# A token's own head of keys and values, by blocks of rows, in a routed attention layer

## The chip, the cores and the metric

The kernel runs on one core of a Trainium2 chip. Its metric is the device time of one execution in microseconds (us); the time before is the median of three runs. One more execution was recorded by the hardware profiler, and its rows are quoted here. PE is the matrix engine (TensorE), PEld its loading of weights, DVE the vector engine, ACT the scalar engine, POOL GpSimd, SP the engine that issues most transfers. SBUF is the on-chip memory, PSUM the accumulators that PE writes to.

## The reference

A decoder of two layers works on `x` of 8 sequences × 256 tokens × 512 features, in float32: 2048 tokens, 16 tiles of 128. After each sublayer comes the residual sum and a layer norm. The first layer has differential attention, a long convolution and a mixture of experts; the second has windows of self attention, cross attention to a context, and the sublayer of this case:

```python
gating = softmax(x @ W_gate.T)                   # 16 gates, one for each head
idx = argmax(gating); indicator = one_hot(idx, 16)
gating_top1 = indicator * max(gating)
q, k, v = split(x @ W_qkv.T, 3)                  # 16 heads of 32 features each
k_shared = einsum('bth,bthd->btd', indicator, k)     # the token's own head of k
v_shared = einsum('bth,bthd->btd', gating_top1, v)   # the same head of v, times its gate
att = einsum('bhqd,bkd->bhqk', q, k_shared) / sqrt(32)
y = einsum('bhqk,bkd->bhqd', softmax(causal(att)), v_shared)
```

Each token has 16 heads of queries, and one head of keys and values, whose number its gate chooses.

## The kernel before

`x` stays in SBUF as 16 tiles of 128 tokens × 512 features. `D` is 512, `KB` = 4 its chunks of 128, `P` = 128; a group is 4 tiles (512 tokens, two sequences), and `NG` = 4 groups are worked off one after another. A matmul 128×512 in float32 runs as two passes, so it has two records in the profile. `project` (L171) and `product_steps` (L182) issue the 4 matmuls of a product; `transpose` (L165) and `turned` (L194) turn a tile by 4 transposes and one copy.

**The mixture of experts** (`experts`) sorts tokens: a router chooses, POOL scatters the rows to a DRAM buffer `xs` by slots that are counted out per expert (L782), PE works on blocks of 128 rows whose expert's weights are addressed by a register (loaded at L915), and the results are gathered.

**Cross attention** (`cross_attention`, L1548 to L1633) does per group: 4 tiles turned, `seven_tokens` (sums of quarters of the turned tokens), three times `seven_products` (q, k, v; 7 products of 4 matmuls 128×256 instead of 8), and then the attention of two sequences, which a pipeline works off in pieces beside the next group's products.

**Routed attention** (`routed_attention`, L1642 to L1739) gives its parts to `causal_attention` (L1097 to L1402), whose order is written out by hand and not by a scheduler. It has 32 units (4 for each sequence, 8 for each group, each unit 4 of the 16 heads). A unit's steps are: `maxima` (12 matmuls `ps_q`, L1151; ACT copies them to `rows`, L1160; POOL masks them, L1162; DVE takes maxima, L1171); 5 units later `weights` (`ps_k`, L1214; ACT's exp to `pT`, L1231; POOL masks and adds, L1232 and L1242); 6 units later `products` (`ps_pv`, L1257 and L1267; DVE's reciprocal L1275 and product L1281). `ps_q` and `ps_k` share one PSUM tile. After a sequence's four maxima, DVE splits them into bfloat16 terms and PE turns them (`ps_n`, L1193). Between these steps `fill` puts pieces of work from a queue sorted by the unit in which they are due, at 0.86 us per matmul (`MM`) and 0.45 per turned tile (`TR`); `need` puts in what is due; `at(slots, place, f)` puts a step at the start, middle or end of a later unit. `begin(g)` calls `prepare` for the next group in the middle of the group before, for group 0 before the first unit.

`prepare` queues per group: 4 tiles turned to `xT`; the gates of the 4 tiles (`ps_g`, 16 matmuls of 16 columns, then DVE's softmax and first maximum); 4 blocks of q (`ps_f`, 16 matmuls 128×512); and for each tile **all 16 heads** of k and of v (`ps_t`, two products of 4 matmuls 128×512). From each `ps_t` DVE picks the token's own head, in `chosen`: a product with the indicator (L1676) and a sum over the heads (L1682). k is repeated four times (L1687) and turned (`keys_turned`, L1692).

Of the kernel before, what the change touches and what calls it, by code (L numbers as in the profile page):

```python
# [16 lines left out]
F32 = mybir.dt.float32  # L17
# [6 lines left out]
P = 128  # L24
# [21 lines left out]
NE = (PH * 2 * P - E * (P - 1) - 1) // P + 1  # L46


@with_exitstack
def decoder_kernel(ctx: ExitStack, tc: tile.TileContext, a: dict, out: bass.AP):  # L50
# [43 lines left out]
    ctx_d = dram.tile([P, KB, B * S], F32, tag="ctx_d", name="ctx_d")  # L94

# [101 lines left out]
    def turned_group(work, pools, g):  # L197

        xT = []

        def step(ti):
            if ti == 0:
                xT.append(work.tile([P, KB, GT], F32, tag="xT", name="xT", bufs=1))
            turned(pools, xT[0][:, :, ti * P : (ti + 1) * P], x[g * TPG + ti])

        return xT, [(0, [(TR, lambda ti=ti: step(ti))]) for ti in range(TPG)]
# [7 lines left out]
    class Pipeline:  # L214
# [3 lines left out]
        def __init__(self):  # L218
            self.steps = []
# [392 lines left out]
    def experts(rt):  # L612
# [480 lines left out]
        return clear_slots, load_experts, load_gu_last, router, blocks, combine, wide  # L1093
# [3 lines left out]
    def causal_attention(name, prepare, finish, upb=KB, gather=None):  # L1097
# [18 lines left out]
        with ExitStack() as st:  # L1116
# [177 lines left out]
            def at(slots, place, f):  # L1294

                if place == "fill":
# [210 lines left out]
    def seven_tokens(work, xT):  # L1507

        (b11, b21), (b12, b22) = quadrants(xT)
        t = work.tile([P, 4, 2, S], F32, tag="ts", name="ts", bufs=1)  # L1510
        nc.vector.tensor_tensor(t[:, 0], b12, b11, ALU.subtract)
        nc.gpsimd.tensor_tensor(t[:, 2], b22, b12, ALU.subtract)
        nc.vector.tensor_tensor(t[:, 1], b22, t[:, 0], ALU.subtract)
        nc.vector.tensor_tensor(t[:, 3], b21, t[:, 1], ALU.subtract)
        return b11, b21, t[:, 1], t[:, 2], t[:, 3], t[:, 0], b22

    def seven_products(work, pools, weights, tokens, dst, token_major=False):
# [3 lines left out]
        def product(n):  # L1521
            ps = pools.tile([P, 2, S], F32, tag="mm", name="ps_7")
            rows, cols = (tokens, weights) if token_major else (weights, tokens)
            for i in range(2):
# [5 lines left out]
                )  # L1530
            return ps
# [4 lines left out]
        p1, u2, u3 = part("p1"), part("u2"), part("u3")  # L1536
# [3 lines left out]
        add(u2, product(2), p1)  # L1540
        add(u3, product(3), u2)
# [6 lines left out]
    def cross_attention(wq, wk, wv, wo):  # L1548
# [52 lines left out]
        with ExitStack() as st:  # L1601
# [7 lines left out]
            for g in range(NG):  # L1609
# [13 lines left out]
                seven_products(work, pools, wq7, x7, lambda i, l: q[l][i])  # L1623
# [3 lines left out]
                seven_products(work, pools, wk7, x7, lambda i, l: k[l][i])  # L1627
                v = work.tile([P, TPG, D], F32, tag="v", name="v_x", bufs=1)
                vq = quadrants(v)
                seven_products(work, pools, wv7, x7, lambda i, l: vq[i][l], True)  # L1630
# [11 lines left out]
    def routed_attention(wqkv, wg):  # L1642

        idx = index_row(const, H1, "idx_h")

        def prepare(work, pools, g, at, here):
# [5 lines left out]
            k4 = work.tile([P, TPG, 4, HD1], F32, tag="k4", name="k4")  # L1652
            ind = work.tile([P, TPG, H1], F32, tag="ind", name="ind")
            itop = work.tile([P, TPG, H1], F32, tag="itop", name="itop")

            def gates():
                ps = pools.tile([P, TPG, H1], F32, tag="mm", name="ps_g")
                for ti in range(TPG):
                    project(
                        ps[:, ti, :],  # L1660
                        lambda k: xT[0][:, k, ti * P : (ti + 1) * P],
                        lambda k: wg[:, k, :],
                    )
                gate = work.tile([P, TPG, H1], F32, tag="gate", name="gate")
                nc.vector.tensor_copy(gate, ps)
                softmax_small(work, gate, H1)
                top = work.tile([P, TPG], F32, tag="top", name="top")
                first_max(work, gate, H1, idx, top, ind)
                nc.vector.tensor_tensor(
                    itop, ind, top.unsqueeze(2).broadcast_to([P, TPG, H1]), ALU.mult  # L1670
                )

            def chosen(dst, ps, by):

                sel = work.tile([P, H1, HD1], F32, tag="sel", name="sel")
                nc.vector.tensor_tensor(  # L1676
                    sel,
                    ps.rearrange("p (h d) -> p h d", d=HD1),
                    by.unsqueeze(2).broadcast_to([P, H1, HD1]),
                    ALU.mult,  # L1680
                )
                nc.vector.tensor_reduce(dst, sel.rearrange("p h d -> p d h"), AX.X, ALU.add)  # L1682

            def key(ti, ps):
                k = k4[:, ti]
                chosen(k[:, 0, :], ps, ind[:, ti, :])
                nc.vector.tensor_copy(k[:, 1:4, :], k[:, 0:1, :].broadcast_to([P, 3, HD1]))  # L1687

            def keys_turned():
                pt = pools.tile([P, TPG, P], F32, tag="mm", name="pt_k")  # L1690
# [6 lines left out]
            xT, need = turned_group(work, pools, g)  # L1697
            need.append((0, [(0.8, gates)]))
            need.append((0, feature_block(pools, qT, xT, wqkv, 0, 0, HD1**-0.5)))
            for ti in range(TPG):  # L1700
                need.append(
                    (0, token_block(pools, xT, wqkv, D, ti, lambda ps, ti=ti: key(ti, ps)))
                )
            for c in range(1, 3):
                need.append((0, feature_block(pools, qT, xT, wqkv, 0, c, HD1**-0.5)))
            need.append((0, [(TR, keys_turned)]))
            for c in range(3, KB):
                need.append((c, feature_block(pools, qT, xT, wqkv, 0, c, HD1**-0.5)))
            for ti in range(TPG):
                need.append(  # L1710
                    (
                        5 + ti // 2 * (4 if g == NG - 1 else 2),
# [142 lines left out]
```

## Time and profile before

| | us |
|---|---|
| median of 3 runs (2217.38 to 2219.33) | 2218.76 |
| the profiled execution, its own time | 2202.62 |
| its span | 2200.8 |
| cross attention | about 1548 to 1843 of the span |
| routed attention, to the first `ps_q` | 1843 to 1876 |
| units 0 to 4 | 1876.0 to 1895.8 |
| units 5 to 12 | 1895.8 to 1975.3 |
| units 13 to 31 | 1975.3 to 2155.3 |
| rest | 2155.3 to 2200.8 |

A page of the profile gives each engine's busy time and share of the span, then the span in 40 slices (a digit is the busy share in tenths). Groups of instructions stand as line, engine, operation, `out<-in` with shapes and count, then busy us, mean ns of one, and the idle time of the engine just before them with what ended it. A timeline's line is start, duration, engine, line and operation, with the idle time before in brackets.

### The profile page before, as it was taken

What the parts mean: (1) busy time and instruction counts of PE and PEld (TensorE: products, weight loads), DVE (VectorE), ACT (ScalarE), POOL (GpSimd) and SP (SyncE); (2) the same over time, 40 slices, a digit from 0 to 9 for tenths busy, and PEclk for the clock granted to TensorE, in tenths of its full rate; (3) what the DMA queues carried; (4) which work ended last, traced back from release to release, by engine and by line L of the source; (5) the groups of instructions that cost most, each with busy time, mean ns of one, the idle gap of its engine ahead of it and who ended that gap; (6) DMA issues with size and microseconds to landing.
All of it is one profiled execution on the core that took longest, in us unless ns stands there. A gap on an engine that the chain in (4) does not pass through costs nothing. (4 is left out here: it accounts for less than half of the span.)

```text
span 2200.8 us, 35612 instructions
## 1 busy us (share of the span) xinstructions
PE 2053.4 (93%) x14904; PEld 1192.7 (54%) x14904; DVE 1272.1 (58%) x1923; ACT 598.9 (27%) x723; POOL 824.4 (37%) x918
## 2 busy tenths in 40 slices
PE   7989899879999999999959999999999999999995
PEld 4545555544453455555524444446877875445543
DVE  4676767758888964222235746466344343476777
ACT  4545545520010013111114333340110110333342
POOL 2566767737556723000033644343000000242343
PEclk9989999989999999999989999999999999999998
DMA  6899801335124144131140201002100100000000
GB/s 221 328 385 382 312 1 45 92 87 198 29 76 164 29 148 149 62 141 61 48 145 29 77 20 58 1 2 96 39 20 20 39 0 1 1 11 11 11 18 33
DMA packets 110032, 197.56 MB, mean 90 GB/s; under 512 B 7088, under 2 KB 30768, under 8 KB 109872
## 3 DMA queue, kind: packets, MB, share of 16 engines
q1 hardware_dynamic: 104752, 178.49, 23.4%
q0 software_dynamic: 5120, 16.78, 2.2%
q8 instruction: 120, 1.97, 0.4%
q14 instruction: 40, 0.33, 0.0%
HBM read 93.54 MB, written 112.20 MB: 93 GB/s over the span
## 5 line engine op out<-in xcount | busy, mean ns | idle before, releaser
L1275 DVE RECIPROCAL rsum<-ps_pv 128x256 f32<-128x256 f32 x128 | 224.4, 1753 | 238.1 <-PE ps_pv L1267 237.9
L171 PE MATMUL ps_y<-kv,wt 128*128 128x512 f32 x640 | 282.6, 600 | 4.4 <-POOL kv L519 3.8
L1231 ACT ACTIVATE pT<-ps_k 128x1536 f32<-128x1536 f32 x128 | 185.7, 1450 | 288.9 <-PE ps_k L1223 286.9
L1171 DVE TENSOR_REDUCE neg<-rows 128x12 f32<-128x1536 f32 x128 | 223.1, 1743 | 50.9 <-POOL rows L1162 50.9
L1160 ACT COPY rows<-ps_q 128x1536 f32<-128x1536 f32 x128 | 184.2, 1439 | 184.0 <-PE ps_q L1151 142.2
L1162 POOL TENSOR_SCALAR_AFFINE_SELECT rows<-rows 128x1024 f32<-128x1024 f32 x128 | 140.1, 1094 | 250.3 <-ACT rows L1160 250.0
L1232 POOL TENSOR_SCALAR_AFFINE_SELECT pT<-pT 128x1024 f32<-128x1024 f32 x128 | 141.1, 1102 | 242.9 <-ACT pT L1231 242.9
L171 PEld LDWEIGHTS ps_y<-kv,wt 128*128 128x128 f32 x640 | 120.9, 192 | 154.4 <-issue 135.8
L1242 POOL TENSOR_TENSOR pT<-pT 128x512 f32<-128x512 f32 x112 | 145.2, 1296 | 9.3
L1077 POOL DMA_INDIRECT w_l1x<-ys,slots x32 | 32.9, 1028 | 267.1 <-DMA ys<-y_m 259.2
L182 PE MATMUL ps_t<-w_l1f,xT 128*128 128x512 f32 x256 | 122.0, 611 | 0.0
L182 PE MATMUL ps_f<-xT,w_l1a 128*128 128x512 f32 x256 | 118.2, 604 | 2.9 <-ACT xT L195 2.9
L992 PE MATMUL po_m<-dn,hT 128*128 (+1 forms) x216 | 101.9, 609 | 1.5
L139 POOL TENSOR_SCALAR rstd<-bn_mv 128x1 f32<-128x1 f32 x80 | 16.9, 212 | 217.0 <-DVE bn_mv L145 211.2
L1267 PE MATMUL ps_pv<-pT,ones_v 128*32 128x256 f32 (+1 forms) x1152 | 85.0, 377 | 6.7 <-POOL pT L1242 6.3
L557 DVE TENSOR_REDUCE yc<-z 128x64 f32<-128x512 f32 x128 | 86.0, 673 | 6.2 <-POOL w_l1a L558 5.8
L1151 PE MATMUL ps_q<-kz,qT 32*128 32x128 f32 x1536 | 62.9, 294 | 22.6 <-ACT pT L1231 17.5
L1151 PEld LDWEIGHTS ps_q<-kT,qT 32*128 32x128 f32 x1536 | 49.9, 190 | 56.2 <-issue 17.0
L1151 PEld LDWEIGHTS ps_q<-kz,qT 32*128 32x128 f32 x1536 | 50.4, 192 | 54.8 <-ACT pT L1231 34.4
L182 PEld LDWEIGHTS ps_f<-xT,w_l1a 128*128 128x128 f32 x256 | 46.3, 189 | 54.8 <-issue 49.3
L1151 PE MATMUL ps_q<-kT,qT 32*128 32x128 f32 x1536 | 62.4, 292 | 12.5 <-ACT kT L1411 4.8
L974 DVE TENSOR_TENSOR h_b<-h_b,pg 128x352 f32<-128x352 f32 x36 | 18.8, 521 | 95.3 <-ACT h_b L973 95.3
(326 smaller groups left out, 3744.6 us busy)
## 6 DMA issues: line engine op xcount, KB each, us to landing
xs<-zero SPq DMA_DIRECT2D x8, 4352.0 KB, 31.3
ys<-zero SPq DMA_DIRECT2D x8, 4352.0 KB, 31.4
filters<-in_L_xattn_k SPq DMA_DIRECT2D x4, 2560.0 KB
first_h<-xs SPq DMA_DIRECT2D x36, 256.0 KB, 2.6
ys<-y_m SPq DMA_DIRECT2D x36, 256.0 KB, 2.0
gu<-in_L_ffn_gate_up_proj SPq DMA_DIRECT2D x3, 2816.0 KB, 19.8
wt<-filters SPq DMA_DIRECT2D x32, 256.0 KB, 2.8
x<-in_x SPq DMA_DIRECT2D x16, 256.0 KB, 4.9
```

The costliest lines, as they stand in the source:

```text
L171: nc.tensor.matmul(ps, lhsT=lhsT(k), rhs=rhs(k), start=(k == 0), stop=(k == n - 1))
L182: nc.tensor.matmul(ps[0], lhsT=lhsT(k), rhs=rhs(k), start=(k == 0), stop=(k == KB - 1))
L557: nc.vector.tensor_reduce(yc[:, lb], z, AX.X, ALU.add)
L992: nc.tensor.matmul(po, lhsT=hT[:m, i, :], rhs=dn[i][:m, bass.ds(e, 1), :], start=(i == 0), stop=(i == len(FCH) - 1),)
L1151: nc.tensor.matmul(block[:, s, j, :], lhsT=q(rows, c, b * S + i * P, P), rhs=k(rows, c, b * S + keys * P, P), start=True, stop=True,)
L1160: nc.scalar.copy(d.rearrange("p j s k -> p s j k"), block)
L1162: nc.gpsimd.affine_select(out=rows, in_=rows, compare_op=ALU.is_ge, fill=-FAR, base=0, pattern=[[0, 8], [-1, P]], channel_multiplier=1,)
L1171: return lambda: nc.vector.tensor_reduce(neg[u // upb % 2][:, :, :, c], d, AX.X, ALU.max, negate=True)
L1231: nc.scalar.activation(p[:, 0:3].rearrange("p j s q -> p s j q"), block, AF.Exp)
L1232: nc.gpsimd.affine_select(out=p[:, 0:2].rearrange("p j s q -> p (j s) q"), in_=p[:, 0:2].rearrange("p j s q -> p (j s) q"), compare_op=ALU ...
L1242: nc.gpsimd.tensor_tensor(p[:, 3], p[:, 1], p[:, 2], ALU.add)
L1275: nc.vector.reciprocal(r, ps[:, 1, :])
```

## The change

Keys and values are no longer formed for all heads. Tokens are sorted by their head in two halves of 8 tiles, as in the mixture of experts: a half's rows go to `xs`, in slots that are filled up to blocks of 128 rows of one head each (8 + 15 = 23 blocks, `NKB`). A block is turned and multiplied by the 64 columns of k and v of its head, which a register selects; the results go to a DRAM buffer `kv_d` and are gathered back by token. A new class `Heads` does this:

- `gate`: a tile's 16 gates, and a copy of them on DVE. `choose`: softmax, first maximum and running sums. `places`: three small matmuls (`ps_pl`) and some 15 small operations on DVE that make slots, and the head of each block.
- `send`: a scatter of a tile on POOL. Only the first half's are declared independent of one another.
- `blocks`: a list of 25 steps, of which step b turns block b+2 (`pt_h`), loads block b's head into a PE register and multiplies block b (`ps_kv`); 8 blocks share a PSUM tile, one copy and one transfer. `ahead` buffers are loaded in advance by SP.
- `gather`: a tile's k and v from `kv_d` on POOL.

The first half runs in cross attention: gates after the k products of groups 1 and 2, `choose`, `places` and `send` after those of group 2, and one step of `blocks(ahead=2)` after each of the 21 products of group 3 (`between`); the four steps that remain and the gathers follow. The second half runs in the units of group 0 of routed attention: gates due in units 1 to 3, `choose` in unit 3, `places` in unit 4, sends in units 5 to 7, blocks (`ahead=5`) due in units 9 to 13, gathers in units 13 to 16. `ps_t` and `chosen` are gone; `keys_turned` repeats k by a copy on ACT and multiplies v by its gate on DVE. In `seven_tokens` a difference is formed in place, on POOL and after another on DVE, and in `seven_products` `u3` takes the buffer of `p1`.

On all engines the order before cross attention is as it was. PE's instruction count, as the compiled orders list it, goes from 4879 to 5335, DVE's from 1867 to 1828, ACT's from 629 to 665, POOL's from 848 to 878.

```diff
+NKB = PH + H1 - 1
...
+    kv_d = [dram.tile([NKB * P, 2 * HD1], F32, tag=f"kv{i}", name=f"kv{i}") for i in range(2)]
...
             def at(slots, place, f):
 
-                if place == "fill":
+
+                if place == "due":
+                    at(slots, "start", lambda: insort(queue, f, key=lambda piece: piece[0]))
+                elif place == "fill":
...
-        t = work.tile([P, 4, 2, S], F32, tag="ts", name="ts", bufs=1)
+        t = work.tile([P, 3, 2, S], F32, tag="ts", name="ts", bufs=1)
         nc.vector.tensor_tensor(t[:, 0], b12, b11, ALU.subtract)
-        nc.gpsimd.tensor_tensor(t[:, 2], b22, b12, ALU.subtract)
         nc.vector.tensor_tensor(t[:, 1], b22, t[:, 0], ALU.subtract)
-        nc.vector.tensor_tensor(t[:, 3], b21, t[:, 1], ALU.subtract)
+        nc.gpsimd.tensor_tensor(b12, b22, b12, ALU.subtract)
+        nc.vector.tensor_tensor(t[:, 2], b21, t[:, 1], ALU.subtract)
...
+            between()
             return ps
...
+                steps = []
+                if g == NG - 1:
+                    steps = half.blocks(work, pools, evacuate, 2)
...
+                if 0 < g < NG - 1:
+                    for ti in range(TPG):
+                        xt = work.tile([P, KB, P], F32, tag="xT_b", name="xT_g")
+                        transpose(pools, xt, x[(g - 1) * TPG + ti], "mm")
+                        half.gate(pools, (g - 1) * TPG + ti, lambda k: xt[:, k, :])
+                if g == NG - 2:
+                    half.choose()
+                    half.places(pools)
+                    half.send(range(PH))
...
-                seven_products(work, pools, wv7, x7, lambda i, l: vq[i][l], True)
+                seven_products(work, pools, wv7, x7, lambda i, l: vq[i][l], True, between)
+                if g == NG - 1:
+                    while steps:
+                        between()
+                    for t in range(PH):
+                        half.gather(t)
...
+        def gate(self, pools, t, xT):
+            ps = pools.tile([P, H1], F32, tag="mm", name="ps_g")
+            project(ps, xT, lambda k: self.wg[:, k, :])
+            nc.vector.tensor_copy(self.logits[:, t - self.first, :], ps)
...
+        def send(self, tiles):
+            for i in tiles:
+                ins = nc.gpsimd.indirect_dma_start(
+                    out=xs[:, :],
+                    out_offset=bass.IndirectOffsetOnAxis(ap=self.slots[:, i : i + 1], axis=0),
+                    in_=x[self.first + i],
+                    in_offset=None,
+                )
+                if self.first == 0:
+                    tc.declare_no_dep(ins.ins, group="heads", reason="every token has its own slot")
+                    tc.add_to_no_dep_group("heads", ins.ins)
...
+        def blocks(self, work, pools, copy, ahead=5):
+            xb, xT, out = {}, {}, []
+            def load(b):
+                if b < NKB:
+                    xb[b] = work.tile([P, D], F32, tag="xb_h", name="xb_h", bufs=ahead)
+                    nc.sync.dma_start(out=xb[b], in_=xs[b * P : (b + 1) * P, :])
+            def turn(b):
+                if b < NKB:
+                    pt = pools.tile([P, KB, P], F32, tag="mm", name="pt_h")
+                    for k in range(KB):
+                        nc.tensor.transpose(pt[:, k, :], xb[b][:, k * P : (k + 1) * P], ident)
+                    xT[b] = work.tile([P, KB, P], F32, tag="xT_b", name="xT_h", bufs=min(3, ahead))
+                    copy(xT[b], pt)
+                    del xb[b]
+                    load(b + ahead)
+            def step(b):
...
+                turn(b + 2)
+                e = nc.values_load(
+                    self.heads[0:1, b : b + 1],
+                    engines=(mybir.EngineType.PE,),
...
+                for k in range(KB):
+                    nc.tensor.matmul(
+                        out[-1][:, b % 8],
+                        lhsT=xT_b[:, k, :],
+                        rhs=self.w[:, k, bass.ds(e, 1)],
+                        start=(k == 0),
+                        stop=(k == KB - 1),
+                    )
+                n = b % 8 + 1
+                if n == 8 or b == NKB - 1:
+                    y = work.tile([P, 8, 2 * HD1], F32, tag="sc", name="kv_b")
+                    copy(y[:, :n], out.pop()[:, :n].rearrange("p b a d -> p b (a d)"))
...
+            return [lambda b=b: step(b) for b in range(-2, NKB)]
...
-            for ti in range(TPG):
-                need.append(
-                    (0, token_block(pools, xT, wqkv, D, ti, lambda ps, ti=ti: key(ti, ps)))
-                )
...
-            for ti in range(TPG):
-                need.append(
-                    (
-                        5 + ti // 2 * (4 if g == NG - 1 else 2),
-                        token_block(
-                            pools, xT, wqkv, 2 * D, ti,
-                            lambda ps, ti=ti: chosen(v[:, ti, :], ps, itop[:, ti, :]),
...
+            if g == 0:
+
+                other = halves[1]
+                other.rows_for(work)
+                for n in range(2, NG):
+                    late[n], turns = turned_group(work, pools, n, f"xT{n}")
+                    for ti, (_, steps) in enumerate(turns):
+                        t = n * TPG + ti
+                        tokens = lambda k, n=n, ti=ti: late[n][0][:, k, ti * P : (ti + 1) * P]
+                        gate = lambda t=t, tokens=tokens: other.gate(pools, t, tokens)
+                        need.append((n - 1 + ti // 2, steps + [(0.9, gate)]))
+                at(3, "mid", other.choose)
+                at(4, "fill", [(0.4, lambda: other.places(pools))])
+                for i in range(PH):
+                    at(5 + i // 3, ("start", "mid", "end")[i % 3], lambda i=i: other.send([i]))
+                steps = other.blocks(work, pools, nc.scalar.copy)
+                for i, f in enumerate(steps):
+                    at(8, "due", (9 + i * 5 // len(steps), [(1.3 if i > 1 else TR, f)]))
+                for i in range(PH):
+                    at(13 + i // 2, ("mid", "end")[i % 2], lambda i=i: other.gather(PH + i))
```

## The prediction

> **What bounds the kernel now.** I read the totals of the page first, then a table of windows by stage, then the groups by tile and shape inside the routed stage, then the waits and the timeline there. The totals:
>
> ```profile
> span 2200.8 us, 35612 instructions
> PE 2053.4 (93%) x14904; PEld 1192.7 (54%) x14904; DVE 1272.1 (58%) x1923; ACT 598.9 (27%) x723; POOL 824.4 (37%) x918
> PE   7989899879999999999959999999999999999995
> ```
>
> PE is busy for 93% of the span, so a matmul less is a gain only if the stage it leaves stays PE-bound, and a matmul more is a loss wherever it is put into a full stage. The windows (columns: length, then busy us and records of PE, PEld, DVE, ACT, POOL; granted PE clock, DMA share, GB/s) are the MoE blocks of layer 0, the end of cross attention, and five parts of the routed stage:
>
> ```profile
> 905.00:1095.00 190.00, 189.34 (x662) 111.89 (x661) 45.82 (x91) 32.92 (x70) 0.00 (x0) 1.00 0.23 81
> 1700.00:1843.00 143.00, 139.87 (x606) 109.37 (x604) 52.76 (x96) 15.83 (x34) 7.69 (x17) 1.00 0.05 15
> 1843.00:1875.00 32.00, 30.50 (x97) 15.71 (x98) 10.88 (x27) 4.58 (x9) 0.00 (x0) 0.95 0.00 1
> 1975.00:2155.00 180.00, 173.45 (x1682) 93.20 (x1674) 131.23 (x179) 63.23 (x60) 67.70 (x70) 0.96 0.04 14
> 2155.00:2201.00 46.00, 24.06 (x382) 14.46 (x378) 34.02 (x49) 10.52 (x8) 16.37 (x23) 0.80 0.09 35
> ```
>
> Every stretch but the tail is full on PE. What fills it in the routed stage, and what DVE does there:
>
> ```profile
> L182 PE MATMUL ps_t<-w_l1f,xT 128*128 128x512 f32 x256 | 122.0, 611 | 0.0
> L1275 DVE RECIPROCAL rsum<-ps_pv 128x256 f32<-128x256 f32 x32 | 56.0, 1751 | 33.5 <-PE ps_pv L1267 33.3
> L1171 DVE TENSOR_REDUCE neg<-rows 128x12 f32<-128x1536 f32 x32 | 55.8, 1742 | 12.5 <-POOL rows L1162 12.5
> L1682 DVE TENSOR_REDUCE k<-sel 128x32 f32<-128x512 f32 x16 | 16.6, 1040 | 0.5
> ```
>
> The 256 records are the two passes of 128 matmuls `ps_t` (16 tiles, k and v, 4 chunks). The records overlap; start to start one matmul takes 0.86 us, so they hold 128×0.86 = 110 us of PE.
>
> **The sum's base.** The profiled execution took 2202.62 us (span 2200.8); the median of the runs is 2218.76, 16.1 us more. I work out a difference against the profiled one and add it to the median.
>
> **Cost of one gate and one block.** The MoE router does what a new gate does, 4 transposes of a tile and 4 matmuls of few columns:
>
> ```profile
> 804.94 0.97 PEld L171 LDWEIGHTS ps_r<-rw,w_l1a 128*128 128x128 f32 x8
> 805.93 0.42 PEld L724 LDWEIGHTS pt_c<-ident,w_l1a 128*128 128x128 f32 x4
> 806.31 0.97 PEld L171 LDWEIGHTS ps_r<-rw,w_l1a 128*128 128x128 f32 x8
> 807.26 0.44 PE L194 MATMUL pt<-ident,first_h 128*128 128x128 f32 x2
> ```
>
> From 805.93 to 807.26 is 1.33 us for both: 0.45 of transposes and 8 weight loads of 0.112, so few columns do not make it shorter. A block of 64 columns is the same form: 1.33 us. It also loads its head into a PE register, as the MoE does 36 times (ns: least, median, most):
>
> ```profile
> L915 PEldq TENSOR_LOAD <-i_ex x36: 297/302/786, 792.5 to 1094.7; - x36
> ```
>
> With 4 register operations of 0.05 that is 0.50 us. In the MoE window above these stand among full PE work and PE is busy 189.34 of 190, so I take them as hidden; if open, a block is 1.83. With turn, copy to SBUF and loads all open it is 0.45+0.9+0.9+0.5 = 2.75.
>
> **Cross attention (+46).** 8 gates and 23 blocks go into a stage where PE was busy 139.87 of 143: 31×1.33 = 41.2. Three `ps_pl` matmuls 0.5, and they stand in PE's order behind DVE's chain of small operations in choose: 2. The 4 steps for which the 21 products have no gap stand alone: each waits for its load (the MoE's 256 KB blocks landed in 2.6 us, a step is 1.33): 2. Hidden: block loads and copies, since a step and a product (1.33+1.73) lie between issue and use, twice; the 8 sends on POOL (0.96 each, busy 7.69 of 143) and gathers (3.6 to landing), needed only in routed attention; the POOL subtraction in seven_tokens that now waits for DVE's. The `u3` that reuses p1's buffer waits for an add already done. Range +41 (no waits) to +58 (23×0.5 open).
>
> **To the first ps_q (−22.5).** 32 us before: 16 `ps_g`, 16 `ps_t`, 12 `ps_f` matmuls. After: 4 tiles turned (1.8) and one feature block (3.44), keys_turned (0.45), 5.7 in all, and the copies that PE waits for, of the last turned tile, q, k four times over and kT (0.6 to 0.9 each with hand-over), 3.8: about 9.5.
>
> **Units 0 to 4 (+23).** Before 19.8 us (1876.0 to 1895.8). They now carry 8 turns and gates of the second half (10.6), the first group's other 12 `ps_f` (10.3) and the rest of the next unit's work; each gate stands on PE behind ACT's copy of its own turn (0.5 plus hand-over, 0.9 in all: 7.2 for 8), `ps_pl` behind choose (2.8). The 10 `ps_t` that stood here are gone (9.0). So 19.8+10.6+10.3+7.2+2.8−9.0 = 41.7, and 1 for the first batch's split and turn, which have less work around them: 42.7. Range +12 (waits covered) to +27.
>
> **Units 5 to 12 (+5.5).** Before 79.5 us (1895.8 to 1975.3). Gone are 33 `ps_t` (65 records of the tile in this window, 28 us); added are 23 blocks (30.6). The sends of this half are not declared independent, so each waits on POOL for the landing of the one before: 2.7 us in the MoE's scatters, whose issues otherwise follow at 1.27 (839.71, 840.98). Behind them in POOL's order stand the selects of `rows` and `pT` (1.10 each), for which DVE's maxima and PE's `ps_pv` wait, and the last send releases the first block load on SP. About 10 us of wait over four units, partly covered. Range −8 to +18.
>
> **Units 13 to 31 (−68).** Before 180 us (1975.3 to 2155.3), PE busy 173.45. Gone are 68 `ps_t` (135 records, 58 us), 32 `ps_g` (two groups, 32×0.112×2 = 7.2) and 8 turned tiles (3.6): PE keeps about 105. Another bound lies close to that: the one score tile passes from `ps_q` (0.95) to ACT's copy (1.44), `ps_k`, ACT's exp (1.45) and back. The timeline of ACT shows four units of the forecast's kind already in this profile, between two groups' products:
>
> ```profile
> 2033.24 1.44 ACT L1160 COPY rows<-ps_q 128x1536 f32<-128x1536 f32 x1 [1.44 <-PE ps_q L1151]
> 2039.34 1.44 ACT L1160 COPY rows<-ps_q 128x1536 f32<-128x1536 f32 x1 [1.28 <-PE ps_q L1151]
> 2045.46 1.44 ACT L1160 COPY rows<-ps_q 128x1536 f32<-128x1536 f32 x1 [1.30 <-PE ps_q L1151]
> 2051.56 1.44 ACT L1160 COPY rows<-ps_q 128x1536 f32<-128x1536 f32 x1 [1.28 <-PE ps_q L1151]
> ```
>
> 6.1 us from copy to copy. DVE needs 1.75+1.74+0.42 per unit and about 1.4 of norms and split, 5.35, less than that. 18 units of 6.2, the products spread over them, are 112. Range −75 (5.85 each) to −55 (6.9).
>
> **Tail (−8).** Before 45.5 us; DVE was late there (PE waited 4.59 us for `terms`), among others with `chosen` for v. Range −10 to −2.
>
> **Sum.** 46−22.5+23+5.5−68−8 = −24: 2218.76−24 = 2195.
>
> A rule of the Trainium skill speaks against it: "DMA: Bandwidth & Descriptors", section "Latency and other measured facts", gives a floor of about 600 ns for a tensor_load. This case's row shows a median of 302 ns on PE. By the page 46 exposed loads would be 27.6 us, an estimate that takes the whole gain; by the row they would be 13.9, and hidden, nothing.
>
> **Rivals.** (1) *Waits covered (faster still).* If the gates' copies, choose and the scatter chain are hidden by the units' other work, units 0 to 12 cost +4 (the low ends) instead of +28.5: −48, 2171. For: PE was busy 78.33 of 80 there and the schedule fills gaps. Against: the order on PE is fixed by hand and a gate stands right behind its turn. (2) *Register work just open.* 46×0.5 = +23, sum −1: 2218, no change. Against: the MoE window. (3) *Slower: a block costs more than its tensor time.* In the MoE a register load came once in 8.4 us of PE work (36 from 792.5 to 1094.7), here once in about 3, and at the four steps that stand alone once in 1.3. At +0.52 per block (24/46) the gain is gone, so this decides from 1.85 a block on; at 2.75 a block, 1.42 more than the forecast's 1.33, the sum is 46×1.42−24 = +41, 2260. (4) *Light units do not speed up*: if DVE or the score chain holds 8 us per unit, −68 becomes −36 and the sum +8, 2227. Against: the units of 6.1 above. (5) *Not what it says*: "singly between products" fails for 4 of 25 steps in the first half; two or three us, inside the terms above.
>
> **How the numbers follow.** Forecast 0.50 (own range −40 to −8: 2179 to 2211), rival 1 0.17, rival 2 0.14, rival 3 0.13, rival 4 0.06, rival 5 inside the forecast. No change means within 0.2% (4.4 us), about what a measurement of this kernel can tell. Rival 2 (−10 to +10) gives 0.04 faster, 0.06 same, 0.04 slower; rivals 3 and 4 0.01 same, 0.18 slower. So faster 0.71, same 0.07, slower 0.22. The range leaves out rival 1's lowest fifth (0.04) and the upper half of 3 and 4 (0.10): 2166 to 2230.
>
> **What would show it.** Cross attention about 46 us longer with PE still at 95% and more; blocks' matmuls `ps_kv` start to start 1.33+1.73 with the product; no `ps_t` from the weights w_l1f; first `ps_q` 10 us into the routed stage; units past 13 at 6 to 6.4 us with PE at 85 to 93% of them. Wrong if PE in the first half's gaps idles over 0.5 us per block, if POOL's sends hold the selects for over 20 us, or if the late units stay above 7 us.

## The result and the profile after

The changed kernel took 2219.56 us (median of 12 runs), the kernel before 2216.43 (12 runs, the first three among them). The ratio is 1.0004, 95% interval 0.9989 to 1.0018: **no change**, where 24 us less were forecast. The profiled execution of the changed kernel has these totals:

```profile
span 2217.6 us, 36803 instructions
PE 2023.1 (91%) x15244; PEld 1219.1 (55%) x15244; DVE 1238.0 (56%) x1900; ACT 625.5 (28%) x768; POOL 855.4 (39%) x954
```

PE was busy for 30 us less than before, and its share fell from 93 to 91%: matmuls went, and the time did not. The span is 16.8 us longer than the one before, but 13.9 us of that lie ahead of cross attention, in code that the change doesn't touch: the last `ACTIVATE` of `pT` in self attention starts at 1488.7 before and at 1502.6 after. So I measure stages from that instruction: to the first copy of `rows` in routed attention, from there to the copies of units 5, 13 and 31, and to the end of the last vector instruction. us:

| | to first `rows` | units 0–5 | 5–13 | 13–31 | tail | sum |
|---|---|---|---|---|---|---|
| before | 387.3 | 19.8 | 79.5 | 180.0 | 40.0 | 706.6 |
| after | 408.5 | 51.5 | 92.6 | 116.3 | 37.9 | 706.8 |
| difference | +21.2 | +31.7 | +13.1 | −63.7 | −2.1 | +0.2 |
| forecast | +23.5 | +23 | +5.5 | −68 | −8 | −24 |

These stages leave out the end, from the last vector instruction to the end of the span: 5.6 us before, 8.2 after, in both profiles of each kernel. (The forecast's tail goes to the end of the span: against its −8 stands +0.5.) It waits for POOL's last DRAIN (line, engine, operation; ns: least, median, most; the most is that DRAIN):

```profile
L1851 POOLq DRAIN  x3: 45/113/5912, 2194.1 to 2200.6; - x3
L2061 POOLq DRAIN  x3: 45/113/8531, 2208.2 to 2217.3; - x3
```

The first row is of the kernel before, with 64 scatters and gathers on POOL in all, the second of the changed kernel, with 96. So the profiles differ by +2.8 us in all. The interval of the ratio goes from −2.4 to +4.0 us: nothing is gained. The table of windows of the kernel after has the same stages (columns: length; busy us and records of PE, PEld, DVE, ACT, POOL; granted PE clock; DMA share; GB/s):

```profile
1502.60:1911.10 408.50, 392.84 (x1955) 313.18 (x1948) 166.87 (x308) 51.75 (x102) 51.56 (x74) 1.00 0.17 51
1911.10:1962.60 51.50, 40.22 (x271) 28.94 (x272) 18.09 (x50) 16.17 (x22) 6.02 (x6) 0.73 0.00 1
1962.60:2055.30 92.70, 79.86 (x889) 58.56 (x888) 38.32 (x47) 41.12 (x51) 36.49 (x36) 0.89 0.32 101
2055.30:2171.50 116.20, 100.81 (x1440) 55.15 (x1440) 97.27 (x116) 59.71 (x52) 74.97 (x77) 0.97 0.07 24
```

Two things stand out in the second and third row, beside the idle time of 11 to 13 us each: a clock of 0.73 and 0.89, where the kernel before had 1.00 and 0.98 in these units:

```profile
1876.00:1895.80 19.80, 17.87 (x157) 8.72 (x157) 12.86 (x15) 8.06 (x7) 5.46 (x5) 1.00 0.00 1
1895.80:1975.30 79.50, 77.83 (x725) 40.88 (x726) 50.65 (x72) 28.73 (x28) 28.58 (x28) 0.98 0.01 5
```

The waits of units 0 to 12 name what PE stood behind (engine, line, awaited; us in total, times, longest):

```profile
PE pt_h L1790 <- DMA xb_h<-xs: 9.0, 1, 9.0
POOL xs L1767 <- DMA xs<-x,slots_h: 8.6, 4, 3.0
PE ps_g L174 <- ACT xT L198: 5.6, 8, 0.7
PE ps_pl L1719 <- DVE all_h L1713: 3.8, 1, 3.8
```

Line by line: the first block of the second half, whose load waits for the last send of POOL's chain; that chain; the eight gates behind ACT's copies; the places behind choose. The windows at the same places show the clock:

```profile
1920.00:1930.00 10.00, 8.55 (x59) 5.79 (x57) 1.36 (x3) 3.11 (x5) 1.09 (x1) 0.84 0.01 2
1930.00:1940.00 10.00, 8.70 (x47) 6.75 (x48) 2.01 (x3) 2.60 (x3) 0.81 (x1) 0.50 0.00 0
1950.00:1960.00 10.00, 5.72 (x48) 4.83 (x49) 8.86 (x29) 3.13 (x6) 2.18 (x2) 0.50 0.01 2
1990.00:2000.00 10.00, 6.57 (x31) 6.20 (x31) 0.00 (x0) 2.34 (x4) 2.16 (x2) 0.50 0.70 212
2000.00:2010.00 10.00, 10.00 (x79) 5.65 (x78) 3.85 (x3) 2.30 (x3) 2.36 (x2) 0.74 0.18 53
```

The last row matters most: PE is busy for all of it, and does its work at three quarters of the speed, after the wait for the block is over. Counted in windows of 2 us, PE ran at half clock for 27 us of units 0 to 5 and 20 us of units 5 to 13; in the kernel before for 0 and 3.

### The profile page after: what moved, and what is told of

It reads as the page before. It is cut to its first block, busy times and chain, and to the rows that moved or that the text cites. A ratio compares the mean times of both kernels' runs of the same rounds, so it can differ in the third digit from the quotient of the medians.

```text
span 2217.6 us, 36803 instructions
## 1 busy us (share of the span) xinstructions
PE 2023.1 (91%) x15244; PEld 1219.1 (55%) x15244; DVE 1238.0 (56%) x1900; ACT 625.5 (28%) x768; POOL 855.4 (39%) x954
## 5 line engine op out<-in xcount | busy, mean ns | idle before, releaser
L1270 PE MATMUL ps_pv<-pT,ones_v 128*32 128x256 f32 (+1 forms) x1152 | 86.7, 384 | 9.2 <-POOL pT L1245 9.1
L1154 PEld LDWEIGHTS ps_q<-kT,qT 32*128 32x128 f32 x1536 | 51.5, 195 | 57.0 <-ACT pT L1234 20.8
L1217 PE MATMUL ps_k<-qT,kT 32*128 32x256 f32 (+1 forms) x1024 | 69.9, 360 | 5.4 <-ACT rows L1163 3.6
```

The lines of the kernel that those rows point to most:

```text
L1154: nc.tensor.matmul(block[:, s, j, :], lhsT=q(rows, c, b * S + i * P, P), rhs=k(rows, c, b * S + keys * P, P), start=True, stop=True,)
L1217: nc.tensor.matmul(block[:, s, at, :], lhsT=k(rows, c, b * S + j * P, P), rhs=q(rows, c, b * S + j * P, P * (2 - j)), start=True, stop=False,)
L1270: nc.tensor.matmul(ps[32 * s : 32 * s + 32, 1, j * P :], lhsT=ones_v, rhs=p[:, 1, s, :] if j else first[:, :, s, :], start=(j == 0), stop= ...
```

## The experiments

The theory: the change's arithmetic is right, and units 0 to 12 lose the gain, by waits of PE on other engines and again by the low clock that comes with them. The rivals: the register load of each block is open; the work is only put off; the low clock has no part. A ratio below is to the kernel before, timed beside it; a stage is from one profile, and the sums leave out the end (8.2 us in each kernel with both halves).

**Gates apart.** A gate stands two turned tiles behind its own turn.

```diff
+                        gates.append((0.9, gate))
+                        due = n - 1 + ti // 2
+                        steps = steps + ([gates.pop(0)] if len(gates) > 2 else [])
+                        need.append((due if due < 3 else 2.9, steps))
-                        need.append((n - 1 + ti // 2, steps + [(0.9, gate)]))
```

> Edit: in units 0 to 4 a tile's gate stands on PE two turned tiles behind its own turn, so it no longer waits for ACT's copy; the matmuls are the same. Changed kernel: units 0 to 5 took 51.5 us, with eight waits of 0.67 to 0.73 us (5.6 in all) and a granted clock of 0.50 to 0.67 from 1924 to 1940. Theory A (waits pull the clock down, so a wait is paid twice): the eight waits go and the clock stays near 1 until choose; units 0 to 5 take 39 to 43 us, the whole 9 to 12 us less. Rival B (only idle time counts): 45 to 47 us, the whole 5 to 6 less, and the low clock stays. Rival C (something else orders the units, such as the choose on DVE): under 3 us.

Ratio to the kernel before 0.9959 (0.9936 to 0.9982). Units 0 to 5 took 37.8 us instead of 51.5, the rest as it was, the sum 692.9. The eight waits of 5.6 us are gone, and with them 17 of the 27 us at half clock: 13.7 us less for 5.6 us of waits. Theory A, and below its 39 to 43 us.

**Blocks one unit later.**

```diff
-                    at(8, "due", (9 + i * 5 // len(steps), [(1.3 if i > 1 else TR, f)]))
+                    at(9, "due", (10 + i * 4 // len(steps), [(1.3 if i > 1 else TR, f)]))
```

> Edit: the second half's blocks are queued from unit 9 and due in units 10 to 13, instead of from unit 8 and due in 9 to 13, so that q blocks of group 1 stand where PE waited 9.02 us for the first block's load; the chain of sends on POOL stays. Theory A (PE stood behind a transfer that the sends' chain released late, and ran at half clock for some 15 us after it): units 5 to 13 take 76 to 82 us instead of 92.6, the whole 10 to 16 us less. Rival B (the work is only put off, the blocks then crowd units 10 to 13 and make those longer, or the sends hold up POOL's selects anyway): 89 to 94 us, the whole within 3 us.

Ratio 1.0004 (0.9984 to 1.0024). Units 5 to 13 fell to 86.5 and the wait for the block vanished, but PE then waited 4.2 us for POOL's `pT` (two waits), which stands behind the sends, and units 13 to 31 rose from 116.3 to 121.2. The sum, 703.1, is 3.7 less, but 2.5 of that lie in units 0 to 5 (49.0), which the edit doesn't touch: the same waits stood there, with 20 us at half clock instead of 27. The edit itself is worth 1 us. Rival B for the whole: the wait can be moved, and it comes back in other places.

**Idle work in the waits.** Transposes of the identity into tiles that are written over afterwards.

```diff
+                for i in range(6):        # ahead of each gate of the second half
+                    nc.tensor.transpose(ps[:, 1 + i % 3, :], ident, ident)
...
+                for i in range(32):       # ahead of the places
+                    nc.tensor.transpose(ps[:, 2 + i % 2, :], ident, ident)
...
+                        for i in range(64):   # ahead of the second half's first block
+                            nc.tensor.transpose(pt[:, i % KB, :], ident, ident)
```

> Edit: PE gets idle work that nobody reads in three places where it waited: 6 transposes of the identity (0.67 us) ahead of each of the second half's 8 gates, 32 (3.6) ahead of the places matmuls, 64 (7.2) ahead of the first block's turn in routed attention. Order, waits on other engines and transfers are the same; no wait is taken away. Theory A (the lower clock after a wait is a cost of its own): with PE kept busy the granted clock stays at 0.9 or more from 1924 to 2010, where it was 0.5 to 0.7 for some 40 us; units 0 to 5 fall from 51.5 to 43 to 47 us, units 5 to 13 from 92.6 to 84 to 88, the whole by 10 to 16 us. Rival B (the clock has no part, the waits are all of it): no gain, or up to 5 us longer by idle work that does not fit into the waits.

In its windows at the same work PE is full and the clock is up:

```profile
1920.00:1930.00 10.00, 9.89 (x83) 7.32 (x82) 1.21 (x3) 3.69 (x5) 1.09 (x1) 1.00 0.01 2
1930.00:1940.00 10.00, 9.91 (x80) 7.32 (x80) 2.18 (x4) 3.34 (x5) 1.09 (x1) 1.00 0.00 0
1980.00:1990.00 10.00, 10.00 (x94) 9.74 (x90) 4.82 (x7) 3.01 (x4) 4.42 (x4) 1.00 0.60 184
1990.00:2000.00 10.00, 10.00 (x116) 6.38 (x114) 3.84 (x3) 4.05 (x6) 2.35 (x2) 1.00 0.35 108
```

Units 0 to 5 took 43.8 us, units 5 to 13 88.5, half clock 3 us in each. More work on PE, no wait on another engine taken away, and 11.8 us less in these two stages: this is the clock alone. The sum is 10.2 us less, 0.5%. The timed runs said less (0.9994, 0.9973 to 1.0015, where the changed kernel has 1.0004), so it was run again:

> The kernel with idle work on PE ahead of the gates, the places matmuls and the first block, once more, since its stages were 10.2 us shorter than the changed kernel's in the profiled execution, and its time 0.1% less. Theory A (the gain holds in each execution): ratio to the kernel before 0.994 to 0.998, stages from the end of self attention 694 to 699 us. Rival B (the clock of the profiled execution of the changed kernel was a chance, and a timed execution gains nothing from the idle work): ratio 0.999 to 1.002, stages 700 to 708.

Ratio 0.9967 (0.9947 to 0.9987), theory A, where the changed kernel beside it has 1.0018 (below); stages 43.7 and 88.3: the same. Its sum, 701.9, lies in the range of rival B: it has 411.7 to the first `rows`, where 10 us more at half clock fell into cross attention, and 119.3 in units 13 to 31, with 17 us at half clock instead of 7. So the gain in units 0 to 13 is there in both profiles, and what a whole execution keeps of it differs.

**No register load.**

```diff
-                        rhs=self.w[:, k, bass.ds(e, 1)],
+                        rhs=self.w[:, k, 0:1],
```

> Edit: every block is multiplied by head 0's columns, without a register load (its output is not the reference's for that). 46 register loads and 184 address operations leave PE. Theory A (the register work lies hidden behind the matmuls, as the step of 3.06 us for a product and a block shows): within 3 us. Rival B (it is open, 0.5 us a block): 15 to 23 us less, cross attention alone 8 to 12 less.

Ratio 0.9997 (0.9979 to 1.0014); 408.2 us to the first `rows` with 23 register loads less. They are hidden, to within 2 us (this profile has 3.4 us more of half clock there). Units 5 to 13 were 6.1 us shorter: PE's wait for the first block was 7.4 us instead of 9.0, and 10 us of that stage were at half clock instead of 20. Units 13 to 31 were 2.4 longer. The sum, 703.0, is 3.8 less, a little more than theory A allowed and far from rival B's 15 to 23.

**Blocks of the first half together**, after the 21 products.

```diff
-                if g == NG - 1:
-                    steps = half.blocks(work, pools, evacuate, 2)
...
-                    while steps:
-                        between()
+                    for f in half.blocks(work, pools, evacuate, 2):
+                        f()
```

> Edit: the 25 steps of the first half's blocks all stand after the 21 products of group 3, none between them. Changed kernel: 408.5 us from the end of self attention to the first rows copy, a product with a block 3.06 us. Theory A (the gaps hide each block's load and copy): alone, with two load buffers, a pair of blocks waits for its loads (2.6 us to landing and the copy), 1.6 to 2.0 us per block instead of 1.33, so 8 to 16 us more before the first rows copy, and the rest as it was. Rival B (the tensor time is all that counts, wherever the blocks stand): within 3 us.

Ratio 1.0116 (1.0090 to 1.0141), 426.2 us to the first `rows`, 17.7 more: more than expected. The timeline of PE in that kernel shows waits for loads and, after the last of them, the slow matmuls:

```profile
1822.50 0.60 PE L1788 MATMUL pt_h<-ident,xb_h 128*128 128x128 f32 x4
1823.46 0.63 PE L1788 MATMUL pt_h<-ident,xb_h 128*128 128x128 f32 x4 [0.35 <-DMA xb_h<-xs]
1827.21 1.09 PE L1788 MATMUL pt_h<-ident,xb_h 128*128 128x128 f32 x4 [3.12 <-DMA xb_h<-xs]
1828.09 1.81 PE L1813 MATMUL ps_kv<-w_l1f,xT_h 128*128 x8
```

A turn takes 1.09 instead of 0.60 and a block 1.81 instead of 1.00. PE waited 6.8 us in all for loads, and the granted clock was 0.64 to 0.85 from 1800 to 1840. The stage had 24 us at half clock instead of 3, which costs 10, and 6 us more of waits for loads: some 16 of the 17.7. Standing singly between products is worth 18 us to the first half.

**The first half alone.** Groups 0 and 1 by blocks, groups 2 and 3 with the code of before (`ps_t` and `chosen`).

> Edit: one half of the change alone. Groups 0 and 1 get k and v by blocks, worked off in cross attention as in the changed kernel; groups 2 and 3 form all heads and choose, as in the kernel before. Theory A (the first half's blocks, in gaps of a stage that stays full of matmuls, bring a gain; the second half's waits in units 0 to 12 lose it again): cross attention to the first rows copy 408 to 409 us, units 0 to 5 14 to 20, units 5 to 13 50 to 58, units 13 to 31 165 to 180, so the whole 10 to 25 us less than the kernel before. Rival B (the loss is the first half's 21 us in cross attention, and the second half pays): the whole 0 to 10 us more than the kernel before.

Ratio 0.9974 (0.9959 to 0.9988); stages 408.2, 25.6, 53.2, 172.9, 40.0, sum 699.8. Half of the change, 7 us of gain, below the low end that I expected. Its end takes 6.9 us, so 5.4 of the 7 are left, which is what the ratio says; units 0 to 5 are 26 us shorter than with the second half's gates and choose in them.

**Three edits together**: gates apart, ACT's copy of k at the start of the unit instead of just ahead of its transposes, and idle work at the places and the first block.

> Edits together: the gates stand two turned tiles behind their turns (as in the first experiment); ACT's copy of k is issued at the start of the unit in which it is turned (for groups 0 and 1 when the group's work begins), not just ahead of PE's transposes; and PE gets idle work ahead of the places matmuls (32 transposes) and ahead of the first block's turn in routed attention (64). Theory A (waits and the low clock after them are the loss): units 0 to 5 34 to 37 us (51.5 in the changed kernel), units 5 to 13 84 to 88 (92.6), units 13 to 31 112 to 116, the whole 20 to 26 us less than the changed kernel and 0.8 to 1.2% under the kernel before. Rival B (the clock and the k copies have no part beyond the first experiment's): within 4 us of that one's 692.9 us from the end of self attention to the last vector instruction.

Ratio 0.9932 (0.9911 to 0.9954), sum 696.4, with 43.0 in units 0 to 5, not the 34 to 37 expected. The profiled execution was the slowest of the six that were timed, 2198.27 us against a median of 2189.99. Its clock fell there though PE had hardly waited:

```profile
1905.00:1912.00 7.00, 6.73 (x60) 4.78 (x58) 0.35 (x2) 3.00 (x4) 1.09 (x1) 1.00 0.00 0
1912.00:1926.00 14.00, 14.00 (x74) 11.40 (x73) 2.36 (x5) 3.68 (x5) 1.09 (x1) 0.52 0.00 1
```

What stood on PE from 1908 were the gates and turns in a run, 16 columns to a matmul. So the next kernel puts a matmul of 512 columns between any two gates:

```diff
+                    (2, [T[3], q[2][0], G[1], T[4], q[2][1], G[2], T[5], q[2][2], G[3], q[2][3]]),
```

> Edits: each of the second half's 8 gates stands between two matmuls of 512 columns of the first group's q blocks (turn, q matmul, gate, in turn), instead of behind its own turn or in a run of gates; the rest as in the kernel with gates apart, early k copies and idle work ahead of the places matmuls and the first block. That kernel kept PE busy for 96% from 1908 to 1926 and still ran at a clock of 0.50 from 1912.8 to 1926. Theory A (a run of matmuls of few columns lets the clock fall even where PE does not wait; wide ones between them keep it up, as products between blocks do in cross attention): clock 0.95 or more over units 0 to 3, units 0 to 5 35 to 38 us (43.0 there), the whole 6 to 9 us less than there, 0.9 to 1.3% under the kernel before. Rival B (the clock falls by chance, wherever these gates stand): a low stretch of 7 to 14 us again in units 0 to 5, and 41 to 45 us.

Units 0 to 5 took 36.5 us without any half clock; the first two windows of routed attention have

```profile
1892.00:1902.00 10.00, 10.00 (x75) 6.75 (x73) 2.01 (x3) 6.04 (x8) 1.54 (x2) 1.00 0.00 1
1902.00:1912.00 10.00, 9.73 (x78) 7.11 (x77) 2.19 (x4) 3.77 (x6) 1.74 (x2) 1.00 0.01 2
```

The sum is 689.6, 17 us under the kernel before (14.4 with the end), the ratio 0.9937 (0.9914 to 0.9959): this version beats both kernels. But in time it is no faster than the kernel ahead of it (0.9932), where 6 to 9 us were expected: that the places of the gates gained anything is shown by one profile of each alone. And a run of gates does not always slow PE down:

> The kernel with the gates two turned tiles behind their turns, once more; its first profile had a clock of 1.00 over its gates and 37.8 us for units 0 to 5. If a run of gates lets the clock fall only when it happens to meet the clock's own rhythm: 37 to 45 us for units 0 to 5, with or without a low stretch. If there is no such chance: 37 to 39 us and no low stretch before the places matmuls.

37.7 us for units 0 to 5, and again no low stretch over the gates: the first kernel with gates apart, which has them in a run too, kept its clock over them in both profiles. In both, 10.2 us at half clock began 2.2 us after the last gate, at the end of a wait of 1.6 us for a copy of `rows`, and ahead of the places matmuls. Why the clock fell over the gates in the other kernel is open.

**The two kernels again.**

> The changed kernel once more. If its stages are its own and no chance: from the end of self attention 704 to 710 us, units 0 to 5 48 to 54 with a clock of 0.5 for 20 us or more of 1920 to 1960, units 5 to 13 86 to 94. If the low clock came by chance: units 0 to 5 42 to 46 and the whole below 700.

> The kernel before once more, to see how far its stages differ from one execution to the next: from the end of self attention to the last vector instruction 704 to 709 us, units 0 to 5 18 to 22, units 5 to 13 78 to 82, units 13 to 31 178 to 183.

The changed kernel had 411.7, 51.3, 91.1, 117.9 and 38.0 us, sum 710.0, with 27 and 14 us at half clock in units 0 to 13; its ratio was 1.0018 (1.0000 to 1.0036). The 3 us more to the first `rows` come from the four steps that stand alone at the end of the blocks: PE waited 1.1 us for a load there instead of 0.6, and the next 10 us were at half clock. The kernel before had 387.2, 19.8, 79.5, 179.9 and 39.9, sum 706.4. The loss in units 0 to 12 is the changed kernel's own and no chance, but single stages of the changed kernel differ by up to 3 us between its two profiles.

**What holds the late units and the tail.** DVE takes 32 of 256 reciprocals.

```diff
-                nc.vector.reciprocal(r, ps[:, 1, :])
+                    nc.vector.reciprocal(r[:, :32], ps[:, 1, :32])
```

> Edit to the changed kernel: in routed attention DVE takes the reciprocal of 32 of 256 sums only and uses it for all (the output is not the reference's for that); 1.75 us of each unit's 5.3 us on DVE become about 0.3. Everything else is the same. Theory A (the vector engine's 1.75 + 1.74 + 0.42 us per unit and the norms hold the late units and the tail): units 13 to 31 fall from 116 to 118 us to 106 to 110, 5.9 to 6.1 per unit, where the score tile's round is the next bound; the tail falls from 38 to 28 to 33. Rival B (the score tile's round between PE and ACT is the bound already): units 13 to 31 within 3 us; the tail 33 to 38.

Ratio 0.9979 (0.9957 to 1.0000). The windows of units 13 to 31 and what follows:

```profile
2048.40:2166.30 117.90, 103.45 (x1440) 56.48 (x1440) 71.41 (x118) 59.63 (x52) 75.14 (x77) 0.94 0.08 24
```

26 us of DVE are gone from this stage (97.27 in the changed kernel), and it took 117.9 us, where the changed kernel took 116.3 and 117.9: DVE does not hold it. The tail took 29.3 instead of 37.9: that is DVE's. Rival B's number for the units, theory A for the tail. That the score tile's round holds the units is not shown by this; see below.

**Choose earlier**, at the start of unit 3, in the version with gates between q matmuls, without idle work at the places.

> Edit to the kernel with gates between q matmuls: choose starts on DVE at the start of unit 3 instead of its middle, ahead of that unit's maxima, and PE gets no idle work ahead of the places matmuls. Theory A (PE's wait for choose and the chain of sends behind it are what is left of the loss): units 0 to 5 33 to 36 us (36.5 there), units 5 to 13 84 to 88 (88.6), the whole 2 to 6 us less than its 689.6. Rival B (choose ahead of the maxima puts off DVE's maxima of units 2 and 3, and with them the split and turn of the first sequence, by as much): within 2 us.

Ratio 0.9951 (0.9934 to 0.9968); units 0 to 5 39.8, units 5 to 13 86.7, so 1.4 us more in these together. Rival B: PE waited 3.2 us for a copy of `rows` and 2.8 for choose, and the clock was half for 10 us from the end of the first of these waits. The sum is 699.2, 9.6 more than there; 5.8 of that lie ahead of the first `rows`, where this profile has 17 us at half clock instead of 7, in code that the edit doesn't touch.

## Why the prediction was right or wrong

**Right: the cost of a block and of cross attention.** +21.2 us against +23.5 to the first `ps_q`, and +24.4 in the second profile. Both terms are right, and not only their sum: the first transposes of routed attention come 44.7 us later, counted from the end of self attention (+46; they start at 1899.23 and 1840.60), and from there to the first `ps_q` it is 23.5 less (−22.5). The timeline of the changed kernel in cross attention:

```profile
1812.68 1.95 PE L174 MATMUL ps<-xT,w_l1x 128*128 128x256 f32 x8
1814.46 0.60 PE L1790 MATMUL pt_h<-ident,xb_h 128*128 128x128 f32 x4
1814.90 1.00 PE L1815 MATMUL ps_kv<-w_l1f,xT_h 128*128 x8
1815.74 1.95 PE L174 MATMUL ps<-ts,w_l1x 128*128 128x256 f32 x8
```

From product to product 3.06 us, the 1.73 + 1.33 of the forecast. The register loads took the 0.30 us of the MoE's (median 302 ns) and lay hidden; the floor of 600 ns that the prediction cites was not seen. The rival "register work just open" gave 2218, near what was measured, for a reason that the kernel without register loads refutes. The rival of dearer blocks falls with the same row.

**Wrong: units 0 to 4, +23 forecast, +31.7 measured.** The waits had been named and sized: gates 7.2 and choose 2.8, together 10.0; measured 5.6 and 3.8, together 9.4. What the step left out is that PE is slower around them. With the same waits filled by idle work the stage took 43.8 us, near the 42.7 of the forecast: the term that failed is the duration of a matmul, taken at full clock. I had read a clock of 0.95 to 1.00 in the full stretches of the kernel before, where PE never waited that often, and no term of the sum has a clock in it. PE was busy for 20 of the 27 us at half clock, so these cost about 10 us, the 8.7 that were missed and a little more.

**Too small: units 5 to 12, +5.5 forecast, +13.1 measured** (range −8 to +18). The chain of sends was named, and its 10 us were called partly covered. Of it, PE paid 9.0 us in one wait for the first block, and then 12 us of slow matmuls, since the 17 us at half clock began in that wait. Keeping the clock up brought the stage to 88.5, +9.0.

**A little short, and for another reason: units 13 to 31, −68 forecast, −63.7 measured.** I took the 6.1 us from copy to copy for the round of the one score tile. But PE was full in such units, in the kernel before (first row) as in the changed one (second); only where PE has little to do does the round show alone (third):

```profile
2033.24:2039.34 6.10, 6.10 (x79) 3.13 (x80) 3.79 (x3) 3.39 (x3) 3.02 (x4) 1.00 0.01 3
2108.47:2114.57 6.10, 6.10 (x79) 3.12 (x80) 5.19 (x4) 3.38 (x3) 3.09 (x4) 1.00 0.14 48
2146.96:2152.30 5.34, 3.35 (x72) 1.96 (x68) 5.24 (x8) 2.89 (x2) 4.51 (x7) 1.00 0.02 3
```

So the round is 5.3 us at most, and 6.1 is what PE's own steps and the pieces filled in between them take. That 18 units of 6.2 came near is luck. DVE does not hold them, as the kernel with fewer reciprocals shows. 18 units of 6.1 are 110. The 6.5 us beyond that are in single units, of which the longest (8.7) has PE's wait of 1.2 us for the copy of k in it; what the others add was not tried.

**Wrong: the tail, −8 forecast, +0.5 measured.** The 45.5 us of the forecast go to the end of the span, so its measure is −2.1 to the last vector instruction and +2.6 behind it. I took DVE's lateness there for work that the change removes. Before, the maxima of unit 31 began 9.8 us after the copy of its `rows` (2165.11 against 2155.28), after it 6.1: DVE gained 3.7, and gave 1.8 back in the steps from these maxima to `ps_n`, where two casts took 1.0 and 1.1 us instead of 0.2; why is open. From `ps_n` to the end of the last vector instruction both kernels take 27 us, a chain of DVE's own steps, which only fewer reciprocals shortened. The 2.6 behind it are POOL's DRAIN, a term that the forecast left out: 32 more scatters and gathers.

So the profiles miss the forecast by 27 us, of which 16 are in units 0 to 12, and the two profiles with idle work gave 12 of those back by the clock alone. 4 are in the late units and 8.5 in the tail; the way to the first `ps_q` was 2 better. My first rival, waits covered, was not reached: it put units 0 to 12 at +4, and the best version still has +26 there, with idle work in the place of the wait for the second half's first block. That version gains 14 us in its stages with the end, 0.6% in its time.

## What to carry to other kernels

Before pricing matmuls that move into a stretch with many small waits, ask what clock they will be granted there: a wait of PE was paid more than twice here, once as idle time and again in slow matmuls after it (5.6 us of waits cost 13.7). Put steps that wait for a load singly between wide products (18 us here); where nothing is left to put between, even idle work paid. That matmuls of few columns need the same is not shown: a run of them kept the clock in two profiles of three. Before a period is read as one chain's round, see whether another engine is full in it. A saving at the end of a program is worth only what the chain that ends last does with it, so follow that chain to its last instruction, and the end of the span behind it, before counting on it.

## What the runs showed of the hardware

- Each stretch at half clock lasted a whole multiple of some 3.4 us: 3.4, 6.8, 10.2, 13.7 or 17.1 us in the routed units of the sixteen profiles, but for the last, which the end of the program cut short. The Trainium skill, "TensorE: Matmul & The Clock Gate", Part 1: The HAM clock gate, gives a free-running window of 3413 ns and a clock of either half or all, which agrees. It puts the fall down to an idle window; here it also came with PE busy, by the records of the profile, for 6.73 of the 7 us ahead of it and for all 14 us in it, and in the changed kernel after waits of 0.7 us (PE busy 5.72 of the 6.77 us up to 1926.77, then 13.7 us at half clock).
- The same code ahead of cross attention, unchanged in all kernels, took 1477 to 1506 us in sixteen profiled executions, while each stage of the kernel before repeated within 0.1 us. In the first profile of the changed kernel, ACT stood still for 8.9 us and DVE for 5.7 near 850, both put down to "remote" in the waits: the profile names none of this core's engines or transfers. That is why a difference of two spans says little here, and why stages were compared.
- POOL's last DRAIN grew with the number of scatters and gathers that POOL had issued: 5.91 us with 64, 7.23 with 80 (the first half alone), 8.53 with 96, the same in all sixteen profiles, that is 0.08 us for each, paid at the end of the program.
